# A perceiver block on one core: the order of the first loads, of the small vectors and of the first tiles' work in the cross attention

## The chip, the cores and the metric

The kernel runs on one core of one Trainium2 chip. The metric is the device time of one execution in microseconds (us); three runs of the kernel before were taken, and their median is the time to compare with. One more execution was taken with the hardware profiler, and all durations below are from it.

## The reference

The block takes `x` (32 sequences of 64 tokens of 512 features), a context of 32 x 256 x 512 and a mask of 32 x 256. Everything is float32. Cut to what matters here:

```python
def _L0_xattn_ref(hidden_states, memory_tokens, memory_mask):
    scores = jnp.einsum('bsd,bmd->bsm', hidden_states, memory_tokens) * scale
    scores = jnp.where(memory_mask[:, None, :], scores, neg_inf)
    attn = jax.nn.softmax(scores, axis=-1)
    readout = jnp.einsum('bsm,bmd->bsd', attn, memory_tokens)
    return jnp.where(valid_b[:, None, None], readout, 0)

x = x + _L0_xattn_ref(_layernorm(x), ctx_2048, mask)          # stage a
x = x + _L0_attn_ref(_layernorm(x), wq_a, ..., wo, bo)        # latent attention, 16 heads
x = x + _L0_ffn_ref(_layernorm(x), up, down, expert, ...)     # feed-forward and its norm
```

In the latent attention, the first step is `q = x @ wq_a.T + bq_a` and `kv = x @ wkv_a.T + bkv_a` (384 + 192 = 576 output columns), with an RMS norm over 384 and over 128 of them and a rotary turn of the last 64. The cross attention and this first step are what the change touches; the rest of the latent attention and the feed-forward follow and stay as they are.

## The kernel before

The kernel is one program with stages. The first stage (called a here, the block `with ExitStack() as pa`) makes the cross attention and the first step of the latent attention for 16 tiles of 128 tokens (two sequences each) in a software pipeline: a loop over `i` from 0 to 17 works at the same time on tile `i` (cross attention up to the softmax), tile `r = i - 1` (readout and residual, second layer norm) and tile `q = i - 2` (first step of the latent attention). In each round, in the order of the program text:

- `load_x(i + 1)`, `load(i + 1)`: the tokens, the two context blocks of 512 KB (`load_cx`) and the mask (`load_mk`, two transfers that repeat 256 bytes over 64 partitions), issued by the SP queue.
- `a_t(i, 0)`, `a_t(i, 1)`: TensorE transposes both blocks (line 347, 8 transposes each, tile `psc`); ScalarE and VectorE copy the result into `cT`.
- `stats(i + 1)`: layer-norm statistics of the next tokens (line 119, `lnst_a`), whose inverse root is a power on GpSimd (line 113, `rs_a`).
- `a_q(q, 0)`, `a_q(q, 1)`: the 576 columns in two halves of 12 matmuls (lines 165 to 167, `pq`), a bias add on VectorE (line 429, `ab`).
- `a_e(r)`, `a_r(r)`: transposes of the softmax (line 391, `pse`), readout matmuls (line 402, `pr`), residual `x1` (line 407), then on GpSimd `xt = x1 + bob` (line 408), which SP stores to `x1_d` (line 409), and the statistics of `x1` (`lnst_b`, `rs_b`).
- `a_p(q)`: squares on ScalarE (line 437) and the inverse root for both RMS norms (`rst_qk`, `rs_qk`).
- `a_xT(i)` (line 360, `psx`), `a_s(i)`: scores (line 372, `pss`), the mask as a large negative number (line 368, `ng`, on GpSimd), softmax.
- `a_z`, `a_x(r)` (line 420, `psy`), `a_k(q)`: scaling by the inverse roots, the transposes of the normed tiles.
- every second round a part of the folding of later weights (`load_raw`, `fold_q`, `fold_o`).

Before the loop, SP loads context and tokens of tile 0, its mask, one block of the weight `wq_a`, then tokens, context and mask of tile 1, then four more weight blocks. `prep_wa(j)` (line 242, `psa`) transposes block `j` of `wq_a`/`wkv_a` and splits it into a high and a low part (lines 133 and 135); blocks 0 to 2 are made at the end of round 0, blocks 3 and 4 at the end of round 1. `load_small` runs at the end of round 0 in the program text: three broadcasts on GpSimd's queue (`ab` twice and `bob`) and seven small transfers on SP's queue (`ck`, `cq`, `qaw`, `kvw`, `bqc`, `bqp` twice).

Each engine works off its instructions in a fixed order. The framework sets that order when it builds the program: mostly that of the text, and an instruction goes ahead where its own estimate says that the other must still wait. `tc.issue_after(ins)`, and the kernel's short form `after(ins)`, pin the instructions inside the block behind `ins` on that engine. Tiles come from pools: `xt` has 3 buffers, `cx` 3 (one per tile of 128 tokens), `ng` 1, the PSUM pool `psM` 3 (`pss`, `pq`, `pr`) and `psT` 5.

Of the kernel before, what the change touches and what calls it, by code (L numbers as in the profile page):

```python
# [9 lines left out]
FP = mybir.dt.float32  # L10
# [3 lines left out]
ALU = mybir.AluOpType  # L14
# [13 lines left out]
NEG = -1.0e30  # L28
# [28 lines left out]

READ_AHEAD, READ_FAR = 5, 9


class Turns:

# [10 lines left out]
def perceiver_block(ctx: ExitStack, tc: tile.TileContext, x, mem, mask, wq_a, bq_a, qnw, wq_b, bq_b,  # L73
                    wkv_a, bkv_a, kvnw, wkv_b, wo, bo, gate, up, down, expert, gamma, beta, cs, out):
    nc = tc.nc
# [23 lines left out]
    ident = pid.enter_context(pool("ident")).tile([P, P], FP, name="ident")  # L99
    make_identity(nc, ident)  # L100

    pows = []

    def rstd(sp, var, eps, nm, scale=None):

        n = var.shape[1]
        t = sp.tile([P, n], FP, tag="rs_t", name=f"rst_{nm}")
        if scale is None:
            nc.vector.tensor_scalar(t, var, eps, None, ALU.add)
        else:  # L110
            nc.vector.tensor_scalar(t, var, scale, eps, ALU.mult, ALU.add)
        r = sp.tile([P, n], FP, tag="rs", name=f"rs_{nm}")
        pows.append(nc.gpsimd.tensor_tensor(r, t, mhalf[:, 0:n], ALU.pow))
        return r

    def ln_stats(sp, src, eps, nm):

        st = sp.tile([P, 6], FP, tag="ln_st", name=f"lnst_{nm}")
        nc.vector.bn_stats(st, src)
# [7 lines left out]
    def after(ins):  # L127
        return tc.issue_after(ins.ins) if ins is not None else ExitStack()
# [41 lines left out]
    with ExitStack() as mla:  # L170
# [25 lines left out]
        with ExitStack() as pa:  # L196
# [14 lines left out]
            ab = wp.tile([P, 576], FP, name="ab")  # L211
            bob = wp.tile([P, D], FP, name="bob")

            def load_small():
                nc.gpsimd.dma_start(ab[:, 0:384], bq_a.partition_broadcast(P))
                nc.gpsimd.dma_start(ab[:, 384:576], bkv_a.partition_broadcast(P))
                nc.gpsimd.dma_start(bob, bo.partition_broadcast(P))
                nc.sync.dma_start(ck, cs[:, 0:128].rearrange("p (a t) -> p a t", a=2))
                nc.sync.dma_start(cq, cs[:, 128:640].rearrange("p (a t) -> p a t", a=2))
                with nc.allow_non_contiguous_dma(reason="small vectors"):  # L220
                    nc.sync.dma_start(qaw, qnw.rearrange("(k p) -> p k", p=P))
                    nc.sync.dma_start(kvw, kvnw.rearrange("(k p) -> p k", p=P))
                    nc.sync.dma_start(bqc, bq_b.rearrange("(h q) -> q h", q=QKD)[0:NOPE, :])
                    for j in range(2):
                        nc.sync.dma_start(bqp[64 * j : 64 * j + 64, :], bqd[NOPE:, j, :])

# [85 lines left out]
            def load_cx(i, b):  # L312
                if b == 0:
                    cxs[i] = cxp.tile([P, 4, D], FP, tag="cx", bufs=3, name=f"cx{i}")
                r0 = (2 * i + b) * M
                nc.sync.dma_start(
                    cxs[i][:, 2 * b : 2 * b + 2, :], mem[r0 : r0 + M, :].rearrange("(t p) d -> p t d", p=P)
                )

            def load_mk(i):  # L320
                mks[i] = sp.tile([P, M], U8, tag="mk", bufs=2, name=f"mk{i}")
                for b in range(2):
                    nc.sync.dma_start(mks[i][64 * b : 64 * b + 64, :], mask[2 * i + b, :].partition_broadcast(64))

            def load(i):
                for b in range(2):
                    load_cx(i, b)
                load_mk(i)

            def stats(i):  # L330
                return ln_stats(sp, xts[i], 1e-5, f"a{i}")

# [32 lines left out]
            def a_s(i, cT, xT):  # L365

                ng = ap.tile([P, M], FP, tag="ng", bufs=1, name=f"ng{i}")
                nc.gpsimd.tensor_scalar(ng, mks.pop(i), -1.0, -NEG, ALU.add, ALU.mult)
                pss = psM.tile([P, M], FP, tag="M", name=f"pss{i}")
                for k in range(NKD):  # L370
                    for b in range(2):
                        nc.tensor.matmul(
                            pss[64 * b : 64 * b + 64, :], xT[:, k, 64 * b : 64 * b + 64], cT[b][:, k, :],
                            start=(k == 0), stop=(k == NKD - 1),
                        )
# [20 lines left out]
            def a_r(i, eT, rv):  # L396

                cx, xt = cxs.pop(i), xts.pop(i)
                pr = psM.tile([P, D], FP, tag="M", name=f"pr{i}")
                for tt in range(2):  # L400
                    for b in range(2):
                        nc.tensor.matmul(
                            pr[64 * b : 64 * b + 64, :], eT[:, tt, 64 * b : 64 * b + 64], cx[:, 2 * b + tt, :],
                            start=(tt == 0), stop=(tt == 1),
                        )
                x1 = ap.tile([P, D], FP, tag="x1", name=f"x1{i}")
                nc.vector.scalar_tensor_tensor(x1, pr, rv, xt, ALU.mult, ALU.add)
                nc.gpsimd.tensor_tensor(xt, x1, bob, ALU.add)
                nc.sync.dma_start(x1_d[i // 2][i % 2], xt)
                return x1, ln_stats(sp, x1, 1e-5, f"b{i}")  # L410

            def a_n(i, x1, mr):
                xn = ap.tile([P, D], FP, tag="xn", name=f"xn2_{i}")
# [17 lines left out]
            def a_p(i, qk):  # L431
# [6 lines left out]
                r = rstd(sp, sq, 1e-6, f"qk{i}")  # L438
                return qk, qn, kn, r[:, 0:1], r[:, 1:2], pows[-1]

            def a_rope(i, qk):
# [31 lines left out]
            load_cx(0, 0)  # L473
            load_x(0)
            load_cx(0, 1)
            load_mk(0)
            raws = [load_wa(0)]
            load_x(1)
            load(1)
            raws += [load_wa(j) for j in range(1, 5)]  # L480
            norm(0, stats(0))
            so, xx, hp = {}, {}, {}
            for i in range(NT + 2):
                q, r = i - 2, i - 1
                do_q, do_r = q >= 0, 0 <= r < NT
                if 1 <= i and i + 1 < NT:
                    load_x(i + 1)
                    load(i + 1)
                if do_q and i % 2 == 0:
                    hp[q // 2] = load_raw(q // 2)  # L490
                if i < NT:
                    cT = [a_t(i, 0), a_t(i, 1)]
                if 1 <= i and i + 1 < NT:
                    mr = stats(i + 1)
                if do_q:
                    qk = ap.tile([P, 576], FP, tag="qk", bufs=1, name=f"qk{q}")
# [2 lines left out]
                if do_r:  # L499
                    ex, rv = so.pop(r)  # L500
                    eT = a_e(r, ex)
                if do_q and i != NT:
                    a_q(q, 1, qk, xh, xl)
                    lat = a_p(q, qk)
                if do_r:
                    x1 = a_r(r, eT, rv)
                if i < NT:
                    xT = a_xT(i)
                if i == NT:
                    a_q(q, 1, qk, xh, xl)  # L510
                    lat = a_p(q, qk)
# [9 lines left out]
                    lat = a_z(q, *lat)  # L521
                if i < NT:
                    so[i] = a_s(i, cT, xT)
                if do_r:
                    xx[r] = a_x(r, xn)
                if do_q:
                    a_k(q, *lat)
                if i < 2:
                    for j in range(3 * i, min(3 * i + 3, 5)):
                        last = prep_wa(j, raws[j])  # L530
                if i == 0:
                    load_small()
                    with tc.issue_after(last[1].ins):
                        mr = stats(1)
                if i + 1 < NT:
                    norm(i + 1, mr)
# [763 lines left out]
```

## Time and profile before

| what | value |
|---|---|
| runs, not profiled | 1127.51, 1127.77, 1130.32 us; median 1127.77 us |
| profiled execution, its own time | 1130.98 us |
| span in its profile (first to last instruction) | 1129.1 us |
| mean granted TensorE clock | 0.987 |
| TensorE matmul busy | 1083.1 us (96% of the span) |
| VectorE, ScalarE, GpSimd busy | 773.4, 547.1, 500.5 us |
| DMA | 256.24 MB, 227 GB/s over the span |

PE is TensorE's matmul side, PEld its weight loads, DVE VectorE, ACT ScalarE, POOL GpSimd, SP the queue that issues most transfers. `psc<-ident,cx` reads: writes tile `psc` from `ident` and `cx`. In a row of the timeline the first number is the start in us, the second the time it took, and in brackets stands how long the engine had been idle before it and what released it. Stage a runs from 0 to about 231 us of the span.

### The profile page before, as it was taken

How to read it: one execution, taken by the hardware profiler on the slowest of the kernel's cores; microseconds unless marked ns; L12 is line 12 of the kernel's file. 1: busy time of each engine (PE TensorE's matmuls, PEld its weight loads, DVE VectorE, ACT ScalarE, POOL GpSimd, SP SyncE). 2: the span in 40 equal slices, each digit the busy share in tenths (PEclk: the TensorE clock that was granted, in tenths of full speed). 3: DMA queues.
4: the chain of work that ended last, by engine and by line, in shares of the span. 5: the costliest groups of instructions: out<-in, count | busy, mean ns of one | idle time of the engine just before them, and what ended most of it. 6: DMA issues, size and time to landing. Idle time of an engine off the chain costs nothing. (4 is left out here: it accounts for less than half of the span.)

```text
span 1129.1 us, 25978 instructions
## 1 busy us (share of the span) xinstructions
PE 1083.1 (96%) x10172; PEld 997.9 (88%) x10172; DVE 773.4 (68%) x1372; ACT 547.1 (48%) x1046; POOL 500.5 (44%) x693
## 2 busy tenths in 40 slices
PE   6899999999999999999989999998989998999996
PEld 4677777679999999999889999998989998999996
DVE  4666666656666666666878866667765578687886
ACT  3344444533433434333556544455656567655552
POOL 2333333326788777865552100002068784055171
PEclk9999999999999999999999999999989998999999
DMA  8667666443676787673498776775765689998961
GB/s 244 198 226 241 201 216 203 132 160 119 250 241 226 251 284 264 240 246 114 137 373 300 240 237 208 242 244 190 234 193 185 222 275 304 309 301 269 297 206 57
DMA packets 196730, 256.24 MB, mean 227 GB/s; under 512 B 18480, under 2 KB 140992, under 8 KB 196608
## 3 DMA queue, kind: packets, MB, share of 16 engines
q1 hardware_dynamic: 192336, 243.54, 66.1%
q10 hardware_dynamic: 3456, 8.39, 2.0%
q0 software_dynamic: 816, 2.65, 0.7%
q8 instruction: 80, 1.31, 0.5%
q14 instruction: 42, 0.34, 0.1%
HBM read 147.45 MB, written 107.09 MB: 225 GB/s over the span
## 5 line engine op out<-in xcount | busy, mean ns | idle before, releaser
L690 DVE SCALAR_TENSOR_TENSOR qe<-pse,bqp,cq 64x256 f32<-64x256 f32 x256 | 123.7, 483 | 82.0 <-PE pse L167 76.3
L1038 PE MATMUL up<-xr,wh_up 128*128 128x256 f32 x896 | 161.1, 284 | 7.1 <-DVE uo L151 3.5
L1038 PEld LDWEIGHTS up<-xr,wh_up 128*128 128x128 f32 x896 | 140.0, 193 | 8.3 <-issue 4.0
L135 DVE TENSOR_TENSOR hl<-c,hl 128x896 fp32r<-128x896 f32 x85 | 96.6, 1138 | 49.4 <-ACT hl L133 49.3
L660 PE MATMUL op<-wh_wo,hl 128*128 128x256 f32 x448 | 125.8, 281 | 4.7 <-DVE hl L135 4.7
L1038 PE MATMUL up<-xr,wl_up 128*128 128x256 f32 x448 | 125.4, 283 | 0.0
L661 PE MATMUL op<-wl_wo,hl 128*128 128x256 f32 x448 | 125.2, 281 | 0.1
L660 PE MATMUL dp<-wh_down,hl 128*128 128x256 f32 x448 | 124.7, 278 | 0.3 <-DVE hl L135 0.3
L661 PE MATMUL dp<-wl_down,hl 128*128 128x256 f32 x448 | 124.4, 278 | 0.0
L133 ACT CAST hl<-c 128x896 fp32r<-128x896 f32 x85 | 80.0, 941 | 84.9 <-PE op L661 46.6
L659 PE MATMUL op<-wh_wo,hl 128*128 128x256 f32 x424 | 119.2, 282 | 0.0
L659 PE MATMUL dp<-wh_down,hl 128*128 128x256 f32 x424 | 117.7, 278 | 0.0
L165 PE MATMUL psq<-qa_hi,qh 128*128 128x256 f32 x384 | 113.1, 295 | 0.0
L166 PE MATMUL psq<-qa_hi,ql 128*128 128x256 f32 x384 | 107.0, 279 | 0.0
L167 PE MATMUL psq<-qa_lo,qh 128*128 128x256 f32 x384 | 107.0, 279 | 0.0
L660 PEld LDWEIGHTS op<-wh_wo,hl 128*128 128x128 f32 x448 | 85.1, 190 | 5.3 <-DVE hl L135 5.3
L1038 PEld LDWEIGHTS up<-xr,wl_up 128*128 128x128 f32 x448 | 86.8, 194 | 0.0
L661 PEld LDWEIGHTS op<-wl_wo,hl 128*128 128x128 f32 x448 | 84.8, 190 | 1.6 <-issue 0.3
L661 PEld LDWEIGHTS dp<-wl_down,hl 128*128 128x128 f32 x448 | 84.4, 188 | 1.0
L660 PEld LDWEIGHTS dp<-wh_down,hl 128*128 128x128 f32 x448 | 84.1, 188 | 0.5 <-DVE hl L135 0.5
L719 ACT ACTIVATE s<-s 128x512 f32<-128x512 f32 x32 | 20.2, 632 | 127.7 <-POOL s L718 127.6
L659 PEld LDWEIGHTS op<-wh_wo,hl 128*128 128x128 f32 x424 | 80.6, 190 | 0.0
(227 smaller groups left out, 3230.9 us busy)
## 6 DMA issues: line engine op xcount, KB each, us to landing
c<-vd SPq DMA_DIRECT2D x58, 448.0 KB, 4.2
cx<-in_ctx SPq DMA_DIRECT2D x32, 512.0 KB, 4.5
vd<-vw SPq DMA_DIRECT2D x30, 512.0 KB, 4.0
hd<-uo SPq DMA_DIRECT2D x105, 128.0 KB, 3.5
hd<-uw SPq DMA_DIRECT2D x23, 512.0 KB, 3.0
dcw<-hd SPq DMA_DIRECT2D x20, 448.0 KB, 6.0
c<-hd SPq DMA_DIRECT2D x19, 448.0 KB, 5.8
vd<-v SPq DMA_DIRECT2D x30, 256.0 KB, 3.8
```

Source lines behind the costliest of these rows:

```text
L133: copy = nc.scalar.copy(hi, src)
L135: return copy, engine.tensor_tensor(lo, src, hi.bitcast(FP), ALU.subtract)
L165: nc.tensor.matmul(ps, ah, bh, start=(j == 0), stop=False)
L166: nc.tensor.matmul(ps, al, bh, start=False, stop=False)
L167: nc.tensor.matmul(ps, ah, bl, start=False, stop=(j == n - 1))
L659: nc.tensor.matmul(ps[s // 2][:, s % 2], h[:, a], wh[:, b], start=(k == 0 and s == 6), stop=False)
L660: nc.tensor.matmul(ps[s // 2][:, s % 2], l[:, a], wh[:, b], start=False, stop=False)
L661: ins = nc.tensor.matmul(ps[s // 2][:, s % 2], h[:, a], wl[:, b], start=False, stop=last)
L690: rope = nc.vector.scalar_tensor_tensor(qe[64 * a : 64 * a + 64, :], pe[r, :], bqp[r, p : p + 1], cq[r, a, :], ALU.add, ALU.mult,)
L719: nc.scalar.activation(s, s, AF.Exp)
L1038: nc.tensor.matmul(ps[s // 2][:, s % 2], w[:, i, kk], xr[b, 2 * kk + low][:, j], start=(first and m == 0), stop=(last and m == len(parts) ...
```

## The change

- Ten transposes of the identity matrix into an unused PSUM tile (`warm_up`) stand ahead of the first context's transposes.
- The first loads get another order: block 0 of the weight ahead of tile 0's mask; then context block (1, 0), tokens 1, context block (1, 1), weight block 1, and only then the mask of tile 1 and the other weight blocks.
- The small vectors are split: the three broadcasts on GpSimd's queue are pinned behind the first `ng` (`bob` first); four small transfers (`ck`, `kvw`, `qaw`, `bqc`) go into round 1, behind the loads of tile 2; `cq` and `bqp` go into round 4.
- The transposes of the weight: block 0 stays at the end of round 0, blocks 1 to 4 are spread over round 1 (behind `a_e`, behind `a_xT`, and two behind `a_s`).
- The context transposes of tile 1 are pinned behind the last score matmul of tile 0.
- In round 1, `stats(2)` moves behind `a_r` and is pinned behind the first statistics of `x1`; `ng` of tile 1 is pinned behind the power of tile 1's statistics.
- In round 2, `a_p(0)` moves behind `a_r`, and its `rst_qk` on VectorE is pinned behind the statistics of tile 1's `x1`.
- In every tile, the add `xt = x1 + bob` (line 408) is pinned on GpSimd behind the power `rs_b` of the same tile.

```diff
+WARM = 10
...
-    def rstd(sp, var, eps, nm, scale=None):
+    def rstd(sp, var, eps, nm, scale=None, pin=None):
...
+        with tc.issue_after(pin.ins) if pin is not None else ExitStack():
...
-            def load_small():
-                nc.gpsimd.dma_start(ab[:, 0:384], bq_a.partition_broadcast(P))
-                nc.gpsimd.dma_start(ab[:, 384:576], bkv_a.partition_broadcast(P))
-                nc.gpsimd.dma_start(bob, bo.partition_broadcast(P))
+            def load_small(behind):
+                with after(behind):
+                    nc.gpsimd.dma_start(bob, bo.partition_broadcast(P))
+                    nc.gpsimd.dma_start(ab[:, 0:384], bq_a.partition_broadcast(P))
+                    nc.gpsimd.dma_start(ab[:, 384:576], bkv_a.partition_broadcast(P))
+
+            def load_vectors():
                 nc.sync.dma_start(ck, cs[:, 0:128].rearrange("p (a t) -> p a t", a=2))
...
+                    nc.sync.dma_start(kvw, kvnw.rearrange("(k p) -> p k", p=P))
+                    nc.sync.dma_start(qaw, qnw.rearrange("(k p) -> p k", p=P))
+                    nc.sync.dma_start(bqc, bq_b.rearrange("(h q) -> q h", q=QKD)[0:NOPE, :])
+
+            def load_turns():
                 nc.sync.dma_start(cq, cs[:, 128:640].rearrange("p (a t) -> p a t", a=2))
...
                     for j in range(2):
                         nc.sync.dma_start(bqp[64 * j : 64 * j + 64, :], bqd[NOPE:, j, :])
...
+            def warm_up(n):
+
+                ps = psM.tile([P, P], FP, tag="M", name="warm")
+                for _ in range(n):
+                    nc.tensor.transpose(ps, ident, ident)
...
-                nc.gpsimd.tensor_scalar(ng, mks.pop(i), -1.0, -NEG, ALU.add, ALU.mult)
+                with after(pows[1] if i == 1 else None):
+                    masks.append(nc.gpsimd.tensor_scalar(ng, mks.pop(i), -1.0, -NEG, ALU.add, ALU.mult))
...
-                nc.gpsimd.tensor_tensor(xt, x1, bob, ALU.add)
+                mr = ln_stats(sp, x1, 1e-5, f"b{i}")
+                with after(pows[-1]):
+                    nc.gpsimd.tensor_tensor(xt, x1, bob, ALU.add)
                 nc.sync.dma_start(x1_d[i // 2][i % 2], xt)
-                return x1, ln_stats(sp, x1, 1e-5, f"b{i}")
+                return x1, mr
...
             load_cx(0, 0)
             load_x(0)
             load_cx(0, 1)
+            warm_up(WARM)
+            raws = [load_wa(0)]
             load_mk(0)
-            raws = [load_wa(0)]
+            load_cx(1, 0)
             load_x(1)
-            load(1)
-            raws += [load_wa(j) for j in range(1, 5)]
+            load_cx(1, 1)
+            raws += [load_wa(1)]
+            load_mk(1)
+            raws += [load_wa(j) for j in range(2, 5)]
...
+                if i == 1:
+                    load_vectors()
+                if i == 4:
+                    load_turns()
...
-                    cT = [a_t(i, 0), a_t(i, 1)]
-                if 1 <= i and i + 1 < NT:
+                    with after(scored[0] if i == 1 else None):
+                        cT = [a_t(i, 0), a_t(i, 1)]
+                if 2 <= i and i + 1 < NT:
                     mr = stats(i + 1)
...
+                if i == 1:
+                    prep_wa(1, raws[1])
                 if do_q and i != NT:
                     a_q(q, 1, qk, xh, xl)
-                    lat = a_p(q, qk)
+                    if i != 2:
+                        lat = a_p(q, qk)
                 if do_r:
                     x1 = a_r(r, eT, rv)
+                if i == 2:
+                    lat = a_p(q, qk, stats_of[f"b{r}"])
+                if i == 1:
+                    with after(stats_of["b0"]):
+                        mr = stats(2)
                 if i < NT:
                     xT = a_xT(i)
+                if i == 1:
+                    prep_wa(2, raws[2])
...
+                if i == 1:
+                    prep_wa(3, raws[3])
+                    prep_wa(4, raws[4])
...
-                if i < 2:
-                    for j in range(3 * i, min(3 * i + 3, 5)):
-                        last = prep_wa(j, raws[j])
                 if i == 0:
-                    load_small()
-                    with tc.issue_after(last[1].ins):
+                    last = prep_wa(0, raws[0])
+                    load_small(masks[0])
+                    with after(last[1]):
                         mr = stats(1)
```

More of the change, by code (lines that the diff above doesn't have):

```diff
@@ L100, in perceiver_block @@
     make_identity(nc, ident)
-    pows = []
-    def rstd(sp, var, eps, nm, scale=None):
+    pows, stats_of = [], {}
+    def rstd(sp, var, eps, nm, scale=None, pin=None):
         n = var.shape[1]
         t = sp.tile([P, n], FP, tag="rs_t", name=f"rst_{nm}")
[L108 to L111, printed above, removed]
+        with tc.issue_after(pin.ins) if pin is not None else ExitStack():
+            if scale is None:
+                nc.vector.tensor_scalar(t, var, eps, None, ALU.add)
+            else:
+                nc.vector.tensor_scalar(t, var, scale, eps, ALU.mult, ALU.add)
         r = sp.tile([P, n], FP, tag="rs", name=f"rs_{nm}")
@@ L118, in ln_stats @@
         st = sp.tile([P, 6], FP, tag="ln_st", name=f"lnst_{nm}")
-        nc.vector.bn_stats(st, src)
+        stats_of[nm] = nc.vector.bn_stats(st, src)
         mv = sp.tile([P, 2], FP, tag="ln_mv", name=f"lnmv_{nm}")
@@ L212, in perceiver_block @@
             bob = wp.tile([P, D], FP, name="bob")
-            def load_small():
-                nc.gpsimd.dma_start(ab[:, 0:384], bq_a.partition_broadcast(P))
-                nc.gpsimd.dma_start(ab[:, 384:576], bkv_a.partition_broadcast(P))
-                nc.gpsimd.dma_start(bob, bo.partition_broadcast(P))
-                nc.sync.dma_start(ck, cs[:, 0:128].rearrange("p (a t) -> p a t", a=2))
+            def load_small(behind):
[4 more added lines that the diff above has]
+            def load_vectors():
+                nc.sync.dma_start(ck, cs[:, 0:128].rearrange("p (a t) -> p a t", a=2))
+                with nc.allow_non_contiguous_dma(reason="small vectors"):
+                    nc.sync.dma_start(kvw, kvnw.rearrange("(k p) -> p k", p=P))
+                    nc.sync.dma_start(qaw, qnw.rearrange("(k p) -> p k", p=P))
+                    nc.sync.dma_start(bqc, bq_b.rearrange("(h q) -> q h", q=QKD)[0:NOPE, :])
+            def load_turns():
                 nc.sync.dma_start(cq, cs[:, 128:640].rearrange("p (a t) -> p a t", a=2))
                 with nc.allow_non_contiguous_dma(reason="small vectors"):
-                    nc.sync.dma_start(qaw, qnw.rearrange("(k p) -> p k", p=P))
-                    nc.sync.dma_start(kvw, kvnw.rearrange("(k p) -> p k", p=P))
-                    nc.sync.dma_start(bqc, bq_b.rearrange("(h q) -> q h", q=QKD)[0:NOPE, :])
                     for j in range(2):
@@ L371, in a_s @@
                     for b in range(2):
-                        nc.tensor.matmul(
+                        scored[i] = nc.tensor.matmul(
                             pss[64 * b : 64 * b + 64, :], xT[:, k, 64 * b : 64 * b + 64], cT[b][:, k, :],
@@ L429, in a_q, with a_p @@
                 nc.vector.tensor_tensor(qk[:, sl], pq, ab[:, sl], ALU.add)
-            def a_p(i, qk):
+            def a_p(i, qk, pin=None):
                 qn = ap.tile([P, QLR], FP, tag="qn", bufs=1, name=f"qn{i}")
@@ L437, in a_p @@
                     nc.scalar.activation(d, t, AF.Square, scale=1.0 / math.sqrt(d.shape[1]), accum_out=sq[:, j : j + 1])
-                r = rstd(sp, sq, 1e-6, f"qk{i}")
+                r = rstd(sp, sq, 1e-6, f"qk{i}", pin=pin)
                 return qk, qn, kn, r[:, 0:1], r[:, 1:2], pows[-1]
@@ L475, in perceiver_block @@
             load_cx(0, 1)
+            warm_up(WARM)
+            raws = [load_wa(0)]
             load_mk(0)
-            raws = [load_wa(0)]
+            load_cx(1, 0)
             load_x(1)
-            load(1)
-            raws += [load_wa(j) for j in range(1, 5)]
+            load_cx(1, 1)
+            raws += [load_wa(1)]
+            load_mk(1)
+            raws += [load_wa(j) for j in range(2, 5)]
             norm(0, stats(0))
-            so, xx, hp = {}, {}, {}
+            so, xx, hp, masks, scored = {}, {}, {}, [], {}
             for i in range(NT + 2):
```

## The prediction

> **What bounds the kernel now.** I read the page first (TensorE's matmul side is busy for 96% of the span), then the busy time by stretches of the start, then who TensorE waits for, then the timeline of the first three tiles. Busy time by stretches: start to end, length, then busy us (and instructions) of PE, PEld, DVE, ACT, POOL, then granted clock, DMA share, GB/s.
>
> ```profile
> 0.00:4.70 4.70, 0.00 (x0) 0.03 (x1) 0.00 (x0) 1.28 (x1) 1.47 (x8) 1.00 0.56 184
> 4.70:15.60 10.90, 8.12 (x41) 6.21 (x41) 2.96 (x6) 2.93 (x5) 2.13 (x4) 1.00 1.00 308
> 15.60:27.60 12.00, 9.05 (x68) 5.91 (x66) 8.55 (x22) 4.70 (x11) 4.01 (x7) 1.00 0.83 202
> 27.60:41.50 13.90, 10.83 (x82) 8.17 (x81) 8.29 (x21) 4.76 (x14) 4.79 (x10) 1.00 0.65 201
> 41.50:45.10 3.60, 3.60 (x20) 3.60 (x19) 1.49 (x5) 3.07 (x9) 0.41 (x2) 0.53 1.00 360
> 45.10:60.00 14.90, 14.70 (x112) 11.50 (x111) 9.84 (x25) 5.62 (x17) 4.95 (x10) 1.00 0.54 174
> ```
>
> From 45.1 on PE idles 0.2 us in 14.9, so a microsecond won earlier moves everything behind it. From 4.70 to 45.10 it is busy 8.12 + 9.05 + 10.83 + 3.60 = 31.60 of 40.40 us: 8.8 us idle, and part of the busy time is at half clock. Who PE waits for, in the first 50 us (total, times, longest):
>
> ```profile
> PE psc L347 <- DMA cx<-in_ctx: 7.5, 2, 4.7
> PE psy L420 <- DVE xn L125: 3.5, 2, 2.4
> PE pss L372 <- ACT xT L362: 1.3, 2, 0.7
> PE psa L242 <- DMA ra<-in_L_attn_wq_a_w: 0.8, 1, 0.8
> PE pr L402 <- ACT eT L393: 0.5, 1, 0.5
> ```
>
> The first context block lands at 4.70, the second at 9.42 (2.8 us of idle). The half clock shows in durations: 8 transposes take 1.94 us at 4.70 and 1.97 at 9.42, where 16 take 1.91 at 17.44. In the weight loads of the scores a pair of rows takes 0.43 us until 14.37 and half of that behind it, so the full clock came at about 14.3. It was lost again at 41.6 and came back at 45.1 (granted 0.53 between), after the wait of 2.4 us that this part of the timeline explains:
>
> ```profile
> 36.64 0.60 DVE L456 TENSOR_SCALAR qn<-qk,rs_qk 128x384 f32<-128x384 f32 x1 [0.88 <-POOL rs_qk L113]
> 37.16 0.74 DVE L407 SCALAR_TENSOR_TENSOR x<-pr,rv,xt 128x512 f32<-128x512 f32 x1
> 38.01 0.68 DVE L119 BATCH_NORM_STATS2 lnst_b<-x 128x6 f32<-128x512 f32 x1
> 39.77 0.55 DVE L125 TENSOR_SCALAR xn<-x,lnmv_b,rs_b 128x512 f32<-128x512 f32 x1 [0.68 <-POOL rs_b L113]
> 40.47 0.63 PE L420 MATMUL psy<-ident,xn 128*128 128x128 f32 x4 [2.40 <-DVE xn L125]
> ```
>
> The readout `pr` ends at 32.92 + 1.94 = 34.86, but the residual `x` starts at 37.16: VectorE sat first behind the RMS norm of tile 0 (`rst_qk`, then `qn` waiting for its power).
>
> **PE's work from the first transposes to 45.1 at full clock.** 16 context transposes are 1.95 us by their start-to-start distance, the four of a square tile 0.5, scores 1.95, readout 1.94, softmax transposes 0.3, 12 matmuls of `pq` 1.6. Four contexts 7.8, two scores and one readout of the first two tiles 5.85, `psx` and `psy` 1.5, weights 2.2, softmax 0.3; tile 2's round: `pq` 3.2, readout and scores 3.9, the small transposes 1.9. Sum 26.6, taken as 26.3 for what overlaps at the joints. So the 31.60 busy us hold 5.3 of half clock: about 3.5 before 14.3 (half of 1.94, of 1.97, of the four-transposes' 1.06 twice, 0.66 of the scores) and 1.8 from 41.6 to 45.1. Before: 26.3 + 5.3 + 8.8 = 40.4.
>
> **The change, part by part.**
>
> *Ten extra transposes.* At half clock 0.21 us each: 2.1 to 2.4 us on PE, between the identity and the first context. The identity is ready at 2.46 now, but GpSimd spends 0.71 us at 1.34 on issuing `ab` ahead of the last step; with that pinned behind `ng` it is ready at about 1.75. So they end at 4.1 (4.9 at worst), against 4.70: free, or 0.2. What they may bring is an earlier full clock. Busy from 1.75 on, the rise could come at 5.25 (3.5 us later, the length of the slow stretch 41.6 to 45.1), or after the 4.9 busy us that it took today (9.42 to 14.3), which with gaps of 0.5 and 0.35 is 7.5; or as late as today. I take 7.6: half-clock loss 1.0 for the first eight and half of 7.0 to 7.6 for the next, 1.3 (0.5 to 3.5).
>
> A row and a rule differ here. From 41.48 to 44.51 PE ran transposes alone, and the clock was full again at 45.1; so transposes count as work in this trace. The Trainium skill, page "TensorE: Matmul & The Clock Gate", section "Part 4: PE-mode transpose", says that the full clock does not engage for transpose mode, which would speak against this change. By that rule the half-clock loss before the scores would stay at about 3.5 us and the gain below would be 2.2 smaller.
>
> *First loads.* The stretch 5.0 to 7.5 moves 105 to 215 GB/s beside some 390 on either side: the mask's 256-byte pieces and the broadcast `ab` (192 KB, 6.7 us to land) run among the context. `ab` goes away and the mask goes behind a weight block, so 1.25 MB (two context blocks and the tokens) at 390 from 2.5 us end at 5.7, plus 0.7 as for the first block: 6.4 at best, 9.42 at worst; I take 7.0. Idle before the second block 0.35 (0 to 2.8). Tile 1's blocks landed by 12.3 and 13.7 (`ck` and `cq` wait for them on SP); with 2.75 MB ahead instead of 3.0 and without `ab`, about 10 and 12. They are wanted at 11.3 and 12.3, behind the scores of tile 0: idle 0.5 (0 to 1.5). The mask of tile 0 lands as late as today (9.9), and its consumer on VectorE comes at 11.3. Tile 2's context, issued at 20.47 today because two tiny transfers hold SP ahead of it (row below), goes out at 12 to 13 and lands by about 20, when its transposes want it. `bob` and `ab`, issued at 10.5 to 12, land 6.5 us later, ahead of 19.5 and 24. Queued behind the three issues on GpSimd (1.9 us) is the power of tile 1's statistics, wanted 3 us later. `cq` and `bqp` in round 4 take some 3 us of SP ahead of `load_raw`; contexts are read a round ahead, so nothing (up to 3 once if that lead is gone).
>
> ```profile
> 16.86 2.91 SPq L225 DMA_DIRECT2D bqp<-in_L_attn_wq_b_b  x2
> 20.47 0.94 SPq L316 DMA_DIRECT2D cx<-in_ctx  x2
> ```
>
> *Weights spread.* The same 20 transposes and copies; they fill waits of round 1 (0.5 for `eT`, 0.7 for `xT`), and the wait of 0.8 for weight block 2 goes. *Round 1's chain*: from the end of `pr` to `psy` today 21.97 to 26.24 = 4.27; without `stats(2)` between (0.6) about 3.4, under which lie `psx`, scores and three weight blocks (3.8). Left in rounds 0 and 1: 0.3 for `xT` of tile 0, 0.5 for `eT`, 0.5 for `xT`, 0.3 at `psy`.
>
> *Round 2's pin.* `x` can start at the end of `pr`; `psy` comes 0.75 + 0.7 + 0.35 + 0.75 + 0.65 = 3.2 later, 3.9 if the power of `rs_qk` (0.70) stands ahead on GpSimd. PE has `psx`, the wait for `xT` (0.7) and the scores, 3.1, so 0.9 idle (0.3, to 2.4 as today). The gaps are then shorter than the one that cost the clock: 1.8 falls to 0 (to 1.8 if not).
>
> *The add behind the power in every tile.* It frees `rs_b` by 0.1 us (67.87 today). It moves the store and so the reload of `xt` by 1.8 to 2.1 us: VectorE waits in order at `lnst_a`, with both adds of `pq` queued behind it. Today it already waits there once:
>
> ```profile
> 74.42 0.69 DVE L119 BATCH_NORM_STATS2 lnst_a<-xt 128x6 f32<-128x512 f32 x1 [1.30 <-DMA xt<-in_x]
> ```
>
> PE still idles only 0.2 us around it (9.80 of 10 busy from 70 to 80), so some 1 us is covered. I take 0.25 us in all (0 to 1.0 in each of 13 tiles).
>
> **Sum.** After: 26.3 + 1.3 + idle (0.35 + 0.5 + 0.3 + 0.5 + 0.5 + 0.3 + 0.9 + 0.7 = 4.05) = 31.65 for what takes 40.4 now: 8.75 less, minus 0.25 = 8.5. Against the profiled execution's own 1130.98 that is 1122.5; it lies 3.2 above the median of 1127.77, so the forecast in those terms is 1119.3. Cheapest ends: 26.3 + 0.5 + 1.7 = 28.5, 11.9 less, 1115.9.
>
> **The rivals.**
>
> *The loads and the clock don't move (0.14).* Context lands at 9.4 whatever the order, and the clock rises late: +2.45 idle, +2.2 half clock, so 3.85 less, 1123.9. For it: the engines are busy for 1.00 of the stretch to 15.6. Against: that stretch moves 308 GB/s where 390 is seen.
>
> *Round 2's pin doesn't do what it says (0.15).* `rst_qk` also needs ScalarE's squares, done at 35.56, so it could land ahead of `x` in effect, or the reload of tokens 3 (VectorE waited 1.9 for it) holds `x`: +1.5 idle and +1.8 clock, 5.2 less, 1122.6. With the rival above as well (0.07): 0.5 less, 1127.2.
>
> *Slower (0.09).* The later reload of `xt` stalls VectorE in tile after tile. With the full 1.0 us in 13 tiles, 13.0 - 8.75 = 4.3 more, 1132.0. It decides from 8.75 / 13 = 0.67 us for a tile. For it: the wait of 1.30 at 74.42. Against: PE was covered then.
>
> **How the numbers follow.** The forecast holds 0.55. A measurement of this kernel tells 0.3% (3.4 us) from no change. Faster by more: the forecast, the pin's rival and most of the loads' rival, 0.81; within: 0.10; slower: 0.09. The range 1115 to 1126 takes in the cheapest end and the two single rivals, and leaves out the slower case, both rivals together and a little below: some 2 in 10.
>
> **What would show it.** Right: second block's transposes at 6.4 to 7.5; 8 transposes in 1.0 us before 10; tile 2's context transposes at about 20.5 instead of 27.62; tile 3's at about 33 instead of 41.48, with the granted clock at 1.00 there; the wait for `xn` at `psy` under 1.2. Wrong: `lnst_a` waiting for `xt` in most tiles, or PE under 9.7 of 10 busy between 50 and 200.

## The result and the profile after

| | before | after |
|---|---|---|
| runs beside each other, median (lowest to highest) | 1129.07 us (1127.51 to 1132.49, 6 runs) | 1142.59 us (1136.43 to 1145.93, 6 runs) |
| profiled execution, its own time | 1130.98 us | 1136.43 us |
| span, mean granted clock | 1129.1 us, 0.987 | 1134.4 us, 0.989 |

The changed kernel is slower: ratio 1.0098, interval 1.0076 to 1.0119, some 11 us where 8.5 us less were forecast, and clear of no change. The profiled execution of after is the fastest of its six, so its trace understates the loss.

Busy time by stretches of after (columns as before; the stretches end at the marks of after: context of tile 1, of tile 2, of tile 3):

```profile
4.43:11.26 6.83, 6.53 (x41) 5.08 (x41) 3.65 (x8) 2.83 (x5) 2.81 (x5) 1.00 1.04 379
11.26:23.14 11.88, 9.47 (x68) 6.42 (x67) 8.87 (x21) 5.34 (x13) 4.09 (x7) 0.94 0.84 225
23.14:37.61 14.47, 12.10 (x81) 8.98 (x80) 8.82 (x20) 5.03 (x12) 5.04 (x9) 0.93 0.88 299
37.61:45.10 7.49, 7.49 (x53) 5.77 (x53) 3.76 (x11) 3.02 (x9) 0.72 (x2) 1.00 0.26 57
45.10:60.00 14.90, 12.56 (x90) 10.71 (x88) 9.56 (x23) 5.85 (x17) 4.91 (x10) 0.89 0.67 218
```

The first stretch did what was forecast: 41 instructions on PE take 6.83 us (10.90 before), and the DMA moves 379 GB/s where it moved 308. But from 45.1 to 60 PE is now busy for 12.56 us of 14.90 and the clock is at 0.89; before it was 14.70 and 1.00. Who PE waits for in the first 50 us (total, times, longest):

```profile
PE psy L438 <- DVE xn L128: 3.4, 2, 2.4
PE psq L281 <- DVE x L423: 2.1, 1, 2.1
...
PE pss L388 <- ACT xT L377: 0.9, 2, 0.7
PE psc L362 <- DMA cx<-in_ctx: 0.6, 1, 0.6
```

The 7.5 us of waiting for the context are 0.6 now. The 3.5 us for `psy` have stayed, and a wait of 2.1 at `psq` is new. The same piece of round 2 that was shown of before, in the timeline of after:

```profile
31.38 0.75 DVE L423 SCALAR_TENSOR_TENSOR x<-pr,rv,xt 128x512 f32<-128x512 f32 x1
32.17 0.69 DVE L122 BATCH_NORM_STATS2 lnst_b<-x 128x6 f32<-128x512 f32 x1
...
33.34 0.55 POOL L116 TENSOR_TENSOR rs_b<-rst_b,mhalf 128x1 f32<-128x1 f32 x1 [1.47 <-DVE rst_qk L112]
33.86 1.26 POOL L426 TENSOR_TENSOR xt<-x,bob 128x512 f32<-128x512 f32 x1
33.93 1.48 DVE L128 TENSOR_SCALAR xn<-x,lnmv_b,rs_b 128x512 f32<-128x512 f32 x1 [0.59 <-POOL rs_b L116]
...
35.46 0.66 PE L438 MATMUL psy<-ident,xn 128*128 128x128 f32 x4 [1.00 <-DVE xn L128]
```

`x` starts ahead of `qn`, as the pin wants it. But `xn`, the scaling of the second norm, takes 1.48 us; before it took 0.55. What is new beside it is the add on GpSimd (line 426), which starts 0.07 us ahead of it. The group of `xn` over the tiles of the steady part (45 to 240 us: min/median/max in ns, first and last start, forms), first of before, then of after:

```profile
L125 DVE TENSOR_SCALAR xn<-x,lnmv_b,rs_b x14: 536/543/547, 55.1 to 230.0; 128x512 f32<-128x512 f32 x14
```
```profile
L128 DVE TENSOR_SCALAR xn<-x,lnmv_b,rs_b x14: 536/1133/1485, 53.1 to 237.4; 128x512 f32<-128x512 f32 x14
```

From tile 3 on, odd tiles take 1.48 and even ones 0.79 (tile 2 still 0.54). In an even tile VectorE has another step first, so that `xn` starts later into the add:

```profile
81.06 1.28 POOL L426 TENSOR_TENSOR xt<-x,bob 128x512 f32<-128x512 f32 x1
81.84 0.79 DVE L128 TENSOR_SCALAR xn<-x,lnmv_b,rs_b 128x512 f32<-128x512 f32 x1
```

From the start of `x` of tile 2 to that of tile 14, twelve tiles, before takes 216.25 - 51.41 = 164.84 us and after 223.56 - 47.91 = 175.65: 10.8 more. After enters this part 3.5 us ahead and leaves it 7.3 behind.

### The profile page after: what moved, and what is told of

Same layout as the page of the kernel before. It is cut to its first block, busy times and chain, and to the rows that moved or that the text cites. A ratio compares the mean times of both kernels' runs of the same rounds, so it can differ in the third digit from the quotient of the medians.

```text
span 1134.4 us, 25998 instructions
## 1 busy us (share of the span) xinstructions
PE 1081.6 (95%) x10182; PEld 995.3 (88%) x10182; DVE 782.9 (69%) x1372; ACT 547.3 (48%) x1046; POOL 504.3 (44%) x693
## 5 line engine op out<-in xcount | busy, mean ns | idle before, releaser
L1076 PE MATMUL up<-xr,wh_up 128*128 128x256 f32 x896 | 157.4, 280 | 7.0 <-DVE uo L154 3.1
L1076 PEld LDWEIGHTS up<-xr,wh_up 128*128 128x128 f32 x896 | 137.0, 189 | 8.0 <-issue 3.3
L138 DVE TENSOR_TENSOR hl<-c,hl 128x896 fp32r<-128x896 f32 x85 | 95.4, 1122 | 48.7 <-ACT hl L136 46.2
L1076 PE MATMUL up<-xr,wl_up 128*128 128x256 f32 x448 | 123.1, 278 | 0.0
```

Of the source, the lines that this page charges most:

```text
L138: return copy, engine.tensor_tensor(lo, src, hi.bitcast(FP), ALU.subtract)
L1076: nc.tensor.matmul(ps[s // 2][:, s % 2], w[:, i, kk], xr[b, 2 * kk + low][:, j], start=(first and m == 0), stop=(last and m == len(parts) ...
```

## The experiments

The expectations name three theories: P, the pinned add runs beside `xn` and holds it; R, the pinned add stores later, so the tokens are reloaded later and `lnst_a` stalls VectorE; O, another part of the change. "Freed" is the changed kernel with the add where it was, "late" the one with the add behind the softmax. The spans of the two profiles of the changed kernel differ by 5.7 us, more than half of it behind stage a's twelve tiles; so ratios of the runs decide, and from the traces only stage a is read. A ratio stands with its 95% interval in brackets. Medians of before were 1131.85, 1131.76, 1131.35 and 1132.73 in the four groups of runs (14, 26, 24 and 20 runs).

### Which part is it: the add freed, the add alone, the add later

The changed kernel once more, for the spread:

> The changed kernel once more, for a second profile and more times. Its runs lay from 1136 to 1146 us and the first profile was of the shortest; this one should show what the longer ones have more of. Every theory expects 1136 to 1146.

Measured 1142.4 us (1142.09 to 1146.18), ratio 1.0095 [1.0066, 1.0123]. Its profile shows the same steady part: `xn` at 1.48 in the odd tiles, twelve tiles in 176.48 us. The start is not the same: the second context block's transposes begin at 7.71 (6.46 in the first profile), the first stretch takes 9.38 us (4.60 to 13.98) instead of 6.83, and the scores of tile 0 run partly at half clock:

```profile
11.32 2.73 PE L388 MATMUL pss<-cT,xT 128*64 128x256 f32 x16
```

So the start that the first profile shows is one of several that this kernel has.

The changed kernel without the pin of the add:

```diff
-                mr = ln_stats(sp, x1, 1e-5, f"b{i}")
-                with after(pows[-1]):
-                    nc.gpsimd.tensor_tensor(xt, x1, bob, ALU.add)
+                nc.gpsimd.tensor_tensor(xt, x1, bob, ALU.add)
                 nc.sync.dma_start(x1_d[i // 2][i % 2], xt)
-                return x1, mr
+                return x1, ln_stats(sp, x1, 1e-5, f"b{i}")
```

> The changed kernel with one part undone: the add of the output bias on GpSimd stands ahead of the statistics again and is pinned behind nothing. Theory P (the add runs beside the scaling of the second norm on VectorE and holds it: 1.48 us instead of 0.55 in the first profile): all rows of that scaling back at 0.55, the wait of PE for it at most 0.2 in odd tiles, time 1121 to 1126, below the kernel before. Theory R (the add comes later, so the reload of the tokens does, and VectorE stalls at their statistics): the same time, by fewer waits for the tokens. Theory O (the loss is in another part of the change): still 1136 to 1146.

Measured 1127.6 us (1125.83 to 1132.52, 10 runs), ratio 0.9964 [0.9947, 0.9982]: 14.8 us less than the changed kernel in the same group, though a little over the 1121 to 1126 expected. `xn` is back at 0.55, and `psy` waits 0.9 us in 6 waits from 45 to 240. All the rest of the change together is a gain.

The kernel before with this pin and nothing else (the same edit the other way round):

> The kernel before with this one part alone: the add behind the power in every tile. P: the scaling at 1.48 in odd and 0.78 in even tiles, 0.9 and 0.2 us more for a tile, 1136 to 1141. R: also slower, with waits of 1 to 2 us for the tokens in most tiles. O: 1126 to 1131.

Measured 1144.33 us (1139.37 to 1145.23), ratio 1.0098 [1.0064, 1.0132]. One pinned instruction makes the whole loss, and more than the 1136 to 1141 expected. Twelve tiles take 172.19 us (164.84 before), and `xn` 1.48 and 0.79 again.

The add and its store pinned behind `rv`, the last GpSimd step of the round's softmax, where it doesn't meet `xn` but stores later still:

```diff
-                with after(pows[-1]):
+                owed.append((i, x1, xt))
...
+            def a_b(behind):
+                i, x1, xt = owed.pop()
+                with after(behind):
                     nc.gpsimd.tensor_tensor(xt, x1, bob, ALU.add)
...
+                if do_r:
+                    a_b(last_rv[0])
```

> The changed kernel with the add put still later: behind the last GpSimd step of the softmax (rv), where no scaling of a norm runs. It tells P from R. P: the scaling at 0.55 everywhere, time near that of the kernel with the add free, 1121 to 1127. R: the reload of the tokens comes some 4 us later than in the changed kernel, waits for them grow in every tile, and the time is above the changed kernel's, 1145 or more.

Measured 1147.21 us (1142.89 to 1153.87), ratio 1.0135 [1.0091, 1.0179]. So R can cost as much as P, if the add is late enough. Here `xn` is 0.55 throughout, and the waits of this kernel from 45 to 240 us (total, times, longest) are:

```profile
DVE lnst_a L122 <- DMA xt<-in_x: 11.8, 9, 3.1
...
PE psy L442 <- DVE xn L128: 15.9, 11, 4.3
```

### P and R apart: a fourth buffer for the tokens

With four buffers a reload doesn't wait for the last store (and `sc` gets one buffer instead of two, for room):

```diff
-                xts[i] = ap.tile([P, D], FP, tag="xt", bufs=3, name=f"xt{i}")
+                xts[i] = ap.tile([P, D], FP, tag="xt", bufs=4, name=f"xt{i}")
...
-                sc = ap.tile([P, M], FP, tag="sc", name=f"sc{i}")
+                sc = ap.tile([P, M], FP, tag="sc", bufs=1, name=f"sc{i}")
```

First the changed kernel with it:

> The changed kernel with a fourth buffer for the tokens (the softmax tile gives up its second buffer for the room), so that the reload no longer waits for the store of the late add. The add still runs beside the scaling. P alone (the held scaling is the whole loss): scaling still 1.48 and 0.78, time unchanged at 1140 to 1146. R alone (the late reload is the whole loss): 1121 to 1127. Both, as the kernel with the later add suggests: between, 1131 to 1138, with no waits for the tokens over 0.3 us and the odd tiles' wait at psy still near 1.05.

Measured 1142.05 us, ratio 1.008 [1.0049, 1.011]. No wait of `lnst_a` is left from 45 to 240 us (4.8 us in 6 waits in after), and only 0.2% has gone, within the intervals. `xn` still takes 1.48 in the odd tiles, and PE's wait for it there is 1.54 (1.05 in after); in the even tiles it takes 0.54. What holds the changed kernel is not the reload.

The late kernel with it:

> The kernel with the still later add, with the same fourth buffer: the add is out of the way of the scaling, and the reload out of the way of the add. If P and R are the two causes, nothing is left: scaling at 0.55, no waits for the tokens, 1121 to 1127. If the later add was slow for another reason (its place on GpSimd or beside other steps of VectorE), 1138 or more.

Measured 1132.27 us, ratio 0.9997 [0.9981, 1.0013]. The late kernel stood 1.7% above the freed one, and 1.4 of it go with the fourth buffer: there the reload was nearly the whole loss. The 1121 to 1127 expected are not reached; what is left against the freed kernel with the same buffers (next) is within the intervals.

The freed kernel with it:

> The kernel with the add free, with the fourth buffer. Its rounds 2 and 3 still waited 3.8 and 3.0 us for the tokens, followed by waits of TensorE. If that is where the rest of the forecast gain went: 2 to 3 us less than with the add free, 1122 to 1126. If it is covered: the same 1126 to 1129.

Measured 1130.13 us, ratio 0.9978 [0.9964, 0.9992]; the freed kernel gains nothing from a fourth buffer, against both expectations (1122 to 1126, or 1126 to 1129). In its trace the wait for the tokens has only moved: `lnst_a` waits 2.54 us until 34.82, now ahead of `xn`, and `psy` waits 3.18.

### How the add holds the scaling: other lengths of the add

The pinned add cut into two halves:

```diff
-                    nc.gpsimd.tensor_tensor(xt, x1, bob, ALU.add)
+                    for h in (slice(0, D // 2), slice(D // 2, D)):
+                        nc.gpsimd.tensor_tensor(xt[:, h], x1[:, h], bob[:, h], ALU.add)
```

> The changed kernel with its pinned add cut into two adds of 256 columns, both behind the power. If the add on GpSimd shuts VectorE's scaling of the second norm out for as long as one instruction of it runs, the scaling gets in between the halves or behind the second: in the odd tiles it ends some 0.3 us behind the end of a half add. With halves of about 0.65 us that is 0.9 to 1.0 if it gets in between, and 1.5 to 1.6 if the second half starts first. In the first case half of the loss goes (ratio 1.003 to 1.006), in the second nothing goes (1.010 to 1.012). If the two only share bandwidth, the scaling stays at 1.48 less what the issue between the halves leaves free, 1.3 to 1.5, ratio 1.009 to 1.011.

The timeline of an odd tile in it:

```profile
66.18 1.59 POOL L427 TENSOR_TENSOR xt<-x,bob 128x256 f32<-128x256 f32 x2
66.25 0.94 DVE L128 TENSOR_SCALAR xn<-x,lnmv_b,rs_b 128x512 f32<-128x512 f32 x1 [0.66 <-POOL rs_b L116]
67.11 0.95 DVE L128 TENSOR_SCALAR xn<-xt,lnmv_a,rs_a 128x512 f32<-128x512 f32 x1
```

`xn` gets in between the halves and takes 0.94 instead of 1.48, and then the second half holds the next scaling (`xn<-xt`, 0.95 instead of 0.54). The time, though, is 1140.43 us, ratio 1.0068 [1.0047, 1.009]: less of the loss went than expected. In the even tiles `xn` now takes 0.93 instead of 0.79, and the add ends later: `lnst_a` waits 9.6 us in 10 waits from 45 to 240.

The pinned add on the first 256 columns alone (the other half of the tokens goes without the bias):

> The changed kernel with the pinned add on the first 256 columns alone (the attention's output bias is left out of the other half of the residual). If the scaling of the second norm ends 0.3 us behind the end of the add whatever its length, it takes about 0.85 instead of 1.48 in the odd tiles and 0.55 in the even ones, psy waits some 0.4 instead of 1.05, and the ratio falls to 1.000 to 1.003. If the slowing is not tied to the add's end, 1.2 to 1.5 remain and the ratio stays over 1.006.

```profile
64.35 0.72 POOL L427 TENSOR_TENSOR xt<-x,bob 128x256 f32<-128x256 f32 x1
64.42 0.94 DVE L128 TENSOR_SCALAR xn<-x,lnmv_b,rs_b 128x512 f32<-128x512 f32 x1 [0.66 <-POOL rs_b L116]
...
65.41 0.66 PE L439 MATMUL psy<-ident,xn 128*128 128x128 f32 x4 [0.51 <-DVE xn L128]
```

1134.14 us, ratio 1.0015 [0.9996, 1.0034]. The scaling ends at 65.36, the add at 65.07: 0.29 us apart. With the whole add of after in round 2 it was 35.41 and 35.12: 0.29 again. In the even tile of after above it is 82.63 and 82.34. The even tiles of the half add, whose add is over when `xn` starts, stand at 0.54. So the scaling is not slowed by a share; in these rows it is finished a fixed 0.29 us behind the GpSimd instruction that started ahead of it, however long that is.

### The other parts, each undone in the freed kernel

Without the ten transposes, first with four token buffers:

> The same without the ten extra transposes. If they bring an earlier full clock: the second block's transposes and those of psx and psa at half clock, 1 to 2.2 us more than with them. If transposes don't count for the clock: no change within 0.5 us.

Measured 1124.85 us, ratio 0.994 [0.9919, 0.996]. Then with three:

> The freed kernel without the ten extra transposes. With four token buffers their removal made the kernel 5 us faster (0.9978 to 0.994), and there the trace put it down to the order on VectorE: lnst_a(4) stood ahead of psy's xn with them and behind it without. If it is that order, chosen anew in each kernel, the three-buffer kernel loses nothing by the removal and may gain or lose 0 to 3 us by the order alone (ratio 0.993 to 0.998), and psx(0) takes 0.6 or 1.06 as the clock happens. If the ten transposes do bring the full clock earlier, as the prediction said (1.3 instead of 3.5 us of half clock), their removal costs 2 us: 1129.5, ratio 0.998.

Measured 1124.94 us, ratio 0.9944 [0.9925, 0.9963], against 0.9964 [0.9947, 0.9982] with them. With four buffers the two intervals lie apart, with three they overlap. PE's first rows show the clock, of the freed kernel:

```profile
7.22 1.97 PE L362 MATMUL psc<-ident,cx 128*128 128x128 f32 x8 [0.94 <-DMA cx<-in_ctx]
8.98 1.06 PE L375 MATMUL psx<-ident,xn 128*128 128x128 f32 x4
9.84 0.91 PE L251 MATMUL psa<-ident,ra 128*128 128x128 f32 x4
10.72 1.95 PE L388 MATMUL pss<-cT,xT 128*64 128x256 f32 x16
```

and without them:

```profile
7.06 1.97 PE L362 MATMUL psc<-ident,cx 128*128 128x128 f32 x8 [0.65 <-DMA cx<-in_ctx]
8.82 1.06 PE L375 MATMUL psx<-ident,xn 128*128 128x128 f32 x4
9.67 1.06 PE L251 MATMUL psa<-ident,ra 128*128 128x128 f32 x4
10.66 2.55 PE L388 MATMUL pss<-cT,xT 128*64 128x256 f32 x16
```

With them the weight block takes 0.15 less and the scores 0.60 less: 0.75 us in this pair of executions. It is not shown that the transposes bring it, since the moment of the full clock moves from one execution to the next, of one kernel too. In the first profile of the changed kernel it was there at `psx`:

```profile
8.10 0.60 PE L375 MATMUL psx<-ident,xn 128*128 128x128 f32 x4
```

In the second it came while the scores ran, behind 11.32 (row above). And in a kernel without the ten transposes (the one with both edits, below) it was there at `psa`:

```profile
9.23 0.60 PE L251 MATMUL psa<-ident,ra 128*128 128x128 f32 x4
```

Both kernels without them have something else in common: `lnst_a` doesn't hold `x` or `xn` on VectorE for long (its longest wait in rounds 1 to 3 is 0.77 us). VectorE's order there is not that of the freed kernel: the framework chose it anew. In the freed kernel it does, in rounds 2 and 3:

```profile
28.82 0.69 DVE L122 BATCH_NORM_STATS2 lnst_a<-xt 128x6 f32<-128x512 f32 x1 [3.83 <-DMA xt<-in_x]
...
41.47 0.70 DVE L122 BATCH_NORM_STATS2 lnst_a<-xt 128x6 f32<-128x512 f32 x1 [3.04 <-DMA xt<-in_x]
...
45.64 0.74 DVE L423 SCALAR_TENSOR_TENSOR x<-pr,rv,xt 128x512 f32<-128x512 f32 x1
...
46.43 0.71 PE L281 MATMUL psq<-rkv,rq 128*128 128x128 f32 x4 [1.91 <-DVE x L423]
```

So the next kernel takes that away alone: the statistics of the tokens in rounds 1 to 3 behind those of `x1`.

```diff
-                if 2 <= i and i + 1 < NT:
+                if 4 <= i and i + 1 < NT:
                     mr = stats(i + 1)
...
-                if i == 1:
-                    with after(stats_of["b0"]):
-                        mr = stats(2)
+                if 1 <= i <= 3:
+                    with after(stats_of[f"b{r}"]):
+                        mr = stats(i + 1)
```

> The changed kernel with the add free (as in the run with the add freed), and with the token statistics of rounds 1 to 3 behind the statistics of x1 (bn_stats of the token tile i+1 is pinned behind lnst_b of round i). In the freed kernel lnst_a waits 3.83 us at 28.82 and 3.04 us at 41.47 for the reload of the tokens, on VectorE ahead of x. If these waits are where the rest of the forecast went, x of rounds 2 and 3 starts at the end of pr, psy waits under 1 us in both, tile 2's context transposes stay near 23 and tile 3's come at 35 to 36; the time is 2 to 4 us under the freed kernel's (1127.6), ratio 0.993 to 0.995. If not (the token is late for its own norm as well, and psx then waits for it), the same as the freed kernel within 1 us, ratio 0.996.

Measured 1124.24 us, ratio 0.9939 [0.9916, 0.9963], as expected, though this interval alone still overlaps that of the freed kernel. The wait of 1.91 at `psq` is 0.23 there, and `psy` waits 0.83 and 0.54. Tile 3's context transposes come at 36.86, later than the 35 to 36 expected, in an execution whose second context block came at 7.84. Both edits together:

> The freed kernel with the token statistics of rounds 1 to 3 behind those of x1 and without the ten extra transposes: the two edits that made the freed kernel faster by 3.4 and by 2.7 us. If each took away the same thing (lnst_a standing on VectorE ahead of x and of the second norm in rounds 2 and 3), they don't add up: 1123 to 1125, ratio 0.993 to 0.995. If the ten transposes cost something by themselves, 1121 to 1122, ratio 0.991 to 0.992.

Measured 1124.66 us, ratio 0.9936 [0.9917, 0.9955]. They don't add up, which speaks for one and the same thing taken away. VectorE's order from 10 to 50 us is the same in the last two kernels, so they are also the cleaner test of the ten transposes: 0.9939 with them, 0.9936 without. The four kernels without the transposes or with the tokens behind (0.9936 to 0.9944) can't be told apart; each beats before by 6 to 7 us, and no kernel of these runs is faster.

Round 2's RMS norm back ahead of `x`, without its pin:

> The freed kernel with round 2's RMS norm back where it was, ahead of x and without its pin. The prediction gave that pin 1.5 us of idle time and 1.8 of clock: by it this one is 3.3 us slower than the freed kernel (ratio 0.999), with qn ahead of x on VectorE in round 2 and a wait of about 2.4 at psy. If lnst_a's wait for the tokens (3.83 at 28.82) holds x there anyway, the pin brings under 1 us and the ratio stays 0.996 to 0.997.

Measured 1128.93 us, ratio 0.9971 [0.995, 0.9991]. In its round 2 `lnst_a` waits 3.39 us until 28.44, `qn` stands ahead of `x` (32.77) and `psy` waits 2.29, as before. In the freed kernel `x` starts at 30.58, `psy` doesn't wait, and tile 3's context transposes come at 35.49 instead of 37.02. So in its round the pin does what it says. But one round later the lead is gone: `lnst_a` waits 3.04 us there (row above) and 0.68 here, and the next `x` starts at 45.64 in both. The clock stayed at 1.00 here behind the wait of 2.29, and fell in the freed kernel behind that of 1.91 (0.50 from 48 to 50). The loss is not one that the intervals tell.

The loads in the old order:

> The freed kernel with the loads in the old order (mask 0, weight block 0, tokens 1, contexts of tile 1; the small vectors, ab and the turns at the end of round 0). By the prediction the second context block comes at 9.4 again (2.4 us), and tile 2's context is issued at 20.5 and wanted at 23: 3 to 4.7 us of wait there. Together 4 to 7 us slower than the freed kernel: about 1132 to 1134, ratio 1.000 to 1.002. If the loads bring nothing that is kept, 0.996.

Measured 1129.64 us, ratio 0.9985 [0.9968, 1.0002]: 2.4 us worse than the freed kernel, less than the 4 to 7 expected, and the intervals overlap. The second context block's transposes come at 8.73 (7.22 in the freed kernel). Over all profiles with the new order they come at 6.44 to 7.84, with the old one at 8.73 to 9.43.

The weights' transposes in the old places:

> The freed kernel with the weights' transposes in the old places, three blocks at the end of round 0 and two at the end of round 1. By the prediction they filled waits of 0.5 (for eT) and 0.7 (for xT) in round 1, and the wait of 0.8 for a weight block goes when they are spread: 1 to 2 us slower than the freed kernel, 1128.5 to 1129.5, ratio 0.998 to 0.999. If TensorE has the next context's transposes for these gaps anyway, no change: 0.996 to 0.997.

Measured 1132.21 us, ratio 0.999 [0.9976, 1.0004]: 2.9 us worse than the freed kernel, more than expected; the two intervals just touch. The first rows of PE show why:

```profile
11.86 1.08 PE L251 MATMUL psa<-ident,ra 128*128 128x128 f32 x4 [2.47 <-DMA ra<-in_L_attn_wq_a_w]
14.11 0.45 PE L251 MATMUL psa<-ident,ra 128*128 128x128 f32 x1 [1.17 <-DMA ra<-in_L_attn_wq_a_w]
14.49 3.68 PE L388 MATMUL pss<-cT,xT 128*64 128x256 f32 x16
```

With the new loads the weight blocks come behind the contexts, so in their old places PE waits for them (2.47 and 1.17), and the scores of tile 0 run at half clock. So once the loads are reordered, the weights' transposes have to move too.

## Why the prediction was wrong, point by point

**The step that failed** is "The add behind the power in every tile". It was priced at 0.25 us in all, and it costs 14.8 us (changed kernel 1142.4, freed 1127.6). The step followed the add only downstream: store, reload of `xt`, `lnst_a`. It left out what VectorE does while the add runs. The rows of an odd tile of before held what was needed:

```profile
66.64 1.28 POOL L408 TENSOR_TENSOR xt<-x,bob 128x512 f32<-128x512 f32 x1
66.68 0.68 DVE L119 BATCH_NORM_STATS2 lnst_b<-x 128x6 f32<-128x512 f32 x1
67.87 0.55 POOL L113 TENSOR_TENSOR rs_b<-rst_b,mhalf 128x1 f32<-128x1 f32 x1
68.45 0.55 DVE L125 TENSOR_SCALAR xn<-x,lnmv_b,rs_b 128x512 f32<-128x512 f32 x1 [0.69 <-POOL rs_b L113]
```

The add ended at 67.92, and `xn` started at 68.45, released by the power. Pinned behind the power, the add starts at the very moment that releases `xn`, so in the odd tiles the two start together, and in the even ones `xn` starts while the add runs. In before the add ran beside `lnst_b` (0.68 there, 0.68 in after without it), so that a neighbour had cost nothing; the neighbour changed.

That an instruction of GpSimd holds one of VectorE is also what the Trainium skill states: page "SBUF — State Buffer", section "Who interferes with whom", has the two engines share a port pair that the one which starts first keeps for its whole instruction, and counts the VectorE tensor-scalar form among those that can ask for it, in its two-port modes. The runs agree: `xn` of 1.48, 0.94 and 0.79 us ends each time 0.29 us behind the end of the add or half add. The prediction did not weigh the change against this rule.

**What it makes of the time.** The freed kernel differs from after by the pin alone. Its twelve tiles take 211.52 - 45.64 = 165.88 us, 9.8 less than after. In this part PE waits in after for `xn` at `psy` 6.6 us (0.9 in the freed kernel), all in the six odd tiles: 1.05 in most of them, 0.15 in before. It waits 1.2 us for `xl`, a later step of VectorE (0), and 2.2 us in three waits for `xh` of ScalarE (0), and it is busy for 0.5 us more. Together with 0.1 at `psq` that is 9.7. The longer `xn` of the even tiles (0.79) makes PE wait for nothing at `psy`. The waits for `xh` stand where ScalarE has `wq` and the softmax ahead of it; in the freed kernel `xh` comes first. That this other order follows from the pin was not tested.

**The rival "slower"** named the same edit, and another mechanism. The late reload exists: in the changed kernel `lnst_a` waits 4.8 us in 6 waits (8.3 in 9 in its second profile). But none of PE's waits in the twelve tiles is put down to it, and without it (four buffers) the runs are only 0.2% lower, within the intervals. It decides only when the add is later still, as the late kernel shows: 1.0135, and 0.9997 with a fourth buffer. The result "slower" so came for a reason that no rival had.

**The gain at the start** was forecast at 8.75 us, and the freed kernel keeps 4.3 (1131.85 to 1127.6). By the terms of the sum:

- *First loads*: the landing was right: the second block's transposes came at 6.44 to 7.84 in the profiles (forecast 7.0). The old order costs 2.4 us in the runs (forecast 2.45 of idle), which agrees but is not clear of zero.
- *Ten transposes*: the term of the clock is not borne out. 2.2 us less at half clock were forecast; the pair of rows above differs by 0.75, and the pair of kernels with the same order on VectorE by nothing in the runs. Transposes alone did bring the full clock again (in after it was there at 8.10, behind nothing but transposes since 1.40), against the rule on transposes that the prediction weighed. But the moment lay between 5 and 13 us in the profiles with the ten transposes: at the early end the half-add kernel, whose first block takes 1.45 us at 4.38 instead of 1.97, at the late end the second profile of the changed kernel. Without them it lay between 9 and 14. No rule for it came out of these runs, so the 6.83 us of the first stretch of after is in part luck.
- *Weights spread*: right in sign, 2.9 us, more than the 1 to 2 that its terms gave: behind the reordered loads the old places wait for the weight blocks.
- *Round 2's pin*: mis-sized. It was given 3.3 us (1.5 idle, 1.8 clock); undoing it costs 0.8, which can't be told from zero. The pin does win 1.5 us in round 2, and the reload of the tokens takes them back in round 3 (`x` at 45.64 with and without it). The rival "Round 2's pin doesn't do what it says" had the reload, but a round too early. And the 1.8 of clock were not there to be won: without the pin the clock stayed at 1.00 behind a wait of 2.29.
- *Not in the sum*: with all of PE's work earlier by some 5 us, the tokens of rounds 2 and 3 are wanted before they are there, and `lnst_a` stands ahead of `x`. Taking that away brings the gain to 6.9 us (0.9939), so about 7 of the forecast 8.75 were reached.

**The signs that were named.** Right in after: the second block at 6.46, eight transposes (`psx` and `psa`) in 1.04 us from 8.10, the clock at 1.00 behind 37.61, and `psy` waiting 1.00 in round 2. In its second profile the first two failed: 7.71, and no full clock before 10. Wrong: tile 2's context transposes at 23.14 (20.5 forecast, 27.62 before), tile 3's at 37.61 (33; 41.48), `psy` waiting 2.36 in round 1, `lnst_a` waiting in 6 of 14 tiles (9 in the second profile), and from 50 to 200 PE busy for 140.71 us of 150, 9.4 of 10 (147.34 before).

## What to carry to other kernels

Before an instruction is pinned behind another, look at what the same event releases on the other engines: the pinned instruction will run beside exactly that, tile after tile. On GpSimd and VectorE, ask of every pair that will overlap whether such a pair is in the trace with an unchanged duration; a neighbour that cost nothing (`lnst_b`) says nothing of another (`xn`). And when a start is made faster, read again who is waited for: what was in time before becomes the first in a queue that must not wait.

## What the runs showed of the hardware

- A GpSimd add of 128 x 512 floats that starts 0.07 us ahead holds a VectorE scaling of the same size until 0.29 us behind its end (0.55 becomes 1.48). Statistics of the same size on VectorE (`lnst_b`, 0.68) and a scaling of 128 x 384 from PSUM (`wq`, 0.59) keep their durations beside the same add: in before both run beside it in the even tiles, in after neither does.
- It goes by the instruction: cut into halves, the add lets the scaling in between (0.94), and the second half takes the next one (0.95).
- A wait of TensorE of some 2 us can cost the clock and need not. It fell after 2.40 in before, 2.36 and 2.06 in after (behind the latter, at 48.71, the four matmuls of `psq` take 1.06 us instead of 0.61) and 1.91 in the freed kernel. It stayed at 1.00 behind 2.29 without round 2's pin and behind 3.18 in the freed kernel with four buffers.
